# Conv stage of a ConvNeXt-MoE kernel: the choice of experts cut into six parts, and gamma of the stored rows on GpSimd

## The chip, the cores and the metric

The kernel runs on one core of one Trainium2 chip. The metric is the time of one execution on the device in microseconds (us). Before the change it is 4985.2 us, the median of ten runs (4977.12 to 5419.1; nine of the ten lie at or below 4990.11).

Five engines of the core run their own streams of instructions side by side: TensorE (PE in the profile, with its weight loads as PEld), VectorE (DVE), ScalarE (ACT), GpSimd (POOL) and SyncE (SP, which only issues transfers here). They meet through semaphores.

## The reference

Two layers; the change touches the first only. What the first layer computes, in short:

```python
x = depthwise_conv_7x7(input, dw_kernel) + dw_bias        # 32 x 128 x 56 x 56
x = transpose(x, (0, 2, 3, 1))                            # T = 100352 tokens of C = 128 channels
x = (x - mean) / sqrt(var + 1e-6) * ln_gamma + ln_beta    # over the channels of a token
logits = xf @ Wg + bg                                     # 8 experts
topv, topi = top_k(logits, 2); wts = softmax(topv)
# tokens in order of their first weight claim places in the experts, capacity 1.25 * T / 8
h = gelu(eb @ W1 + b1); y = h @ W2 + b2                   # 128 -> 512 -> 128 in each expert
out = input + x + layer_scale * (the two experts' rows, weighted)
```

The second layer (a dilated 3x3 convolution with batch norm, attention on a Fourier transform, gates) follows on that result.

## The kernel before

**Stages.** The conv stage comes first, roughly 0 to 824 us of the span; then the ranking of the tokens, the experts, the return of their rows, and the second layer. Only the conv stage is touched.

**Tiling.** The 100352 tokens are cut into eight groups of 98 columns (`TG`) of 128 tokens. A group's conv result is the SBUF tile `y`, 128 partitions x 98 columns x 128 channels, in float32; there are two of them, so group g + 2 writes where group g lay. One group is convolved in 16 steps (`NS`) of eight channels, each in two halves of four. A half loads its input `xt` on SP's queue (L148; five buffers), runs 32 conv matmuls on TensorE into a PSUM bank `psa` (L157; one of eight banks), and VectorE moves the bank to `y` and adds the bias (L165, called the evacuation). The weights of nine steps stay in SBUF (`stay`), those of the other seven (`wt`) are loaded again for each group (L151).

**What rides along.** All other work on group g is issued among the steps of group g + 1. A group has six blocks of 16 columns and one of two. Each block passes through these phases:

- `stats` (L179): 16 bn_stats (L182), five small VectorE operations (L186 to L192), Sqrt on ScalarE (L193), reciprocal (L194), and the bias `nb` of the normalisation (L195)
- `norm` (L199): 16 activations on ScalarE (L208); in the last group every second one is on VectorE (L203)
- `across` (L219): 16 transposes on TensorE (L225), four evacuations on ScalarE with gamma and beta (L227)
- `affine` (L213): gamma over the block's rows (L214), on VectorE, in the last group on GpSimd; then the store of the rows to `xf` in HBM (L217), 1 MB, issued on ScalarE's queue, in the last group on SP's. Beta is not added here
- `logits` (L234): four matmuls with `Wg` (L237), each for a quarter of the array's columns, and a copy on ScalarE (L246)
- `back` (L248): four transposes (L251) and an addition of the bias on VectorE into `lg` (L254); the small block has L265 and L274 for both phases

`choose` (L283) takes the two best of the eight logits for all 98 columns, and their weights. For each of the two ranks: highest logit (L293), where it is (L294), times reversed index (L297), first such expert (L300); between the ranks the first expert is taken out (L302, L305). Then difference of the two (L316), Exp on ScalarE (L317), and the weights (L318 to L324). These are 16 VectorE instructions and one activation, and ScalarE loads the table of Exp ahead of it and that of Sqrt behind it.

**What sets the order.** `plan` (L332) gives each phase of block b the step min(2b, 11) + d of the next group, with d from `BEHIND` = 0, 1, 3, 4, 4, 6; `choose` comes last, at step 18. There are 16 steps, so what is planned at 16 and later is issued between two groups. In the last group the multiplies and stores are issued behind the steps (`NS` in L340). The Tile framework then places the instructions on the engines and puts in the semaphores, so the order on an engine is near the order of issue, not equal to it. A new group's first evacuation must wait until the stores of the `y` that it overwrites have landed.

Of the kernel before, what the change touches and what calls it, by code (L numbers as in the profile page):

```python
# [30 lines left out]
F32 = mybir.dt.float32  # L31
I32 = mybir.dt.int32
AF = mybir.ActivationFunctionType
ALU = mybir.AluOpType
AX = mybir.AxisListType
# [24 lines left out]
BIG = 1.0e30  # L60
# [14 lines left out]
def conv_seq_kernel(ctx: ExitStack, tc: tile.TileContext, t: dict, out: bass.AP, dbg: dict):  # L75
    nc = tc.nc
# [41 lines left out]
    firsts = [rk.tile([128, FW], F32, name=f"first{r}") for r in (1, 2)]  # L118
    w1, w2 = [rk.tile([128, FW], F32, name=f"w{r}") for r in (1, 2)]

    TG = 2 * NP
    with tc.tile_pool(name="a1", bufs=1) as a1, tc.tile_pool(name="a2", bufs=2) as a2, tc.tile_pool(
        name="a4", bufs=4
    ) as a4, tc.tile_pool(
        name="a5", bufs=5
# [13 lines left out]
        def conv(g, c0, y):  # L139

            stayed = c0 // CB in stays
            if stayed:
                wts = [w[:, stays.index(c0 // CB)] for w in stay]
            else:
                wts = [a2.tile([k, CB, P8 * P8], F32, name=f"wt{b}") for b, k in enumerate(PKS)]
            for c4 in range(0, CB, CX):
                xt = a5.tile([PK, CX, 4 * NCB * NB], F32, name="xt")
                nc.sync.dma_start(out=xt, in_=t["x8"][g, c0 // CB][:, c4 : c4 + CX])  # L148
                if c4 == 0 and (g == 0 or not stayed):
                    for b in range(2):  # L150
                        nc.sync.dma_start(out=wts[b], in_=t[f"wt{b}"][c0 // CB])  # L151
                xv = xt.rearrange("k c (h n q) -> k c h n q", h=2, n=2)
                ps = bank("psa")
                for c in range(4):
                    for b in range(2):
                        for h in range(2):
                            nc.tensor.matmul(  # L157
                                ps[h * 64 : (h + 1) * 64, c * TG : (c + 1) * TG],
                                lhsT=wts[b][:, c4 + c, :],
                                rhs=xv[: PKS[b], c, h, :, b * NB : b * NB + NP],  # L160
                                start=(b == 0),
                                stop=(b == 1),
                            )
                cs = slice(c0 + c4, c0 + c4 + 4)
                nc.vector.tensor_tensor(  # L165
                    out=y[:, :, cs],
                    in0=ps[:, : 4 * TG].rearrange("p (c t) -> p t c", c=4),
                    in1=dwbB[:, cs].unsqueeze(1).broadcast_to([128, TG, 4]),
                    op=ALU.add,
                )  # L170

        def block(g, y, lg, t0, n, end):
# [38 lines left out]


            def affine():  # L213
                (nc.gpsimd if end else nc.vector).tensor_tensor(  # L214
                    out=yb, in0=yb, in1=gB.unsqueeze(1).broadcast_to([128, n, C]), op=ALU.mult
                )
                (nc.sync if end else nc.scalar).dma_start(out=xfv[:, g * TG + t0 : g * TG + t0 + n, :], in_=yb)  # L217

            def across():  # L219
# [40 lines left out]
            else:  # L260
# [12 lines left out]
                def back():  # L273
# [4 lines left out]
                        op=ALU.add,  # L278
                    )

            return [stats, norm, across, affine, logits, back]

        def choose(g, lg):  # L283

            cut = slice(g * TG, (g + 1) * TG)
            bE = [128, TG, E]
            tops = []
            cand = a1.tile(bE, F32, name="cand", tag="cand")
            for r in range(2):

                top = a2.tile([128, TG], F32, name=f"top{r}", tag=f"top{r}")
                first = firsts[r][:, cut]
                nc.vector.tensor_reduce(out=top, in_=lg, axis=AX.X, op=ALU.max)  # L293
                nc.vector.tensor_tensor(  # L294
                    out=cand, in0=lg, in1=top.unsqueeze(2).broadcast_to(bE), op=ALU.is_equal
                )
                nc.vector.tensor_tensor(  # L297
                    out=cand, in0=cand, in1=revi.unsqueeze(1).broadcast_to(bE), op=ALU.mult
                )
                nc.vector.tensor_reduce(out=first, in_=cand, axis=AX.X, op=ALU.max)  # L300
                if r == 0:
                    nc.vector.tensor_tensor(  # L302
                        out=cand, in0=cand, in1=first.unsqueeze(2).broadcast_to(bE), op=ALU.is_equal
                    )
                    nc.vector.scalar_tensor_tensor(  # L305
                        out=lg.rearrange("p t e -> p (t e)"),
                        in0=cand.rearrange("p t e -> p (t e)"),
                        scalar=-BIG,
                        in1=lg.rearrange("p t e -> p (t e)"),
                        op0=ALU.mult,  # L310
                        op1=ALU.add,
                    )
                tops.append(top)

            m1, e1 = tops
            nc.vector.tensor_tensor(out=e1, in0=e1, in1=m1, op=ALU.subtract)  # L316
            nc.scalar.activation(e1, e1, AF.Exp)  # L317
            nc.vector.tensor_scalar(out=e1, in0=e1, scalar1=1.0, scalar2=None, op0=ALU.min)  # L318
            nc.vector.tensor_scalar(out=m1, in0=e1, scalar1=1.0, scalar2=None, op0=ALU.add)
            nc.vector.reciprocal(m1, m1)  # L320
            nc.vector.tensor_scalar(
                out=w1[:, cut], in0=m1, scalar1=0.5, scalar2=1.0, op0=ALU.max, op1=ALU.min
            )
            nc.vector.tensor_tensor(out=w2[:, cut], in0=e1, in1=w1[:, cut], op=ALU.mult)  # L324

        NS = C // CB
        BEHIND = 0, 1, 3, 4, 4, 6
        sizes = [16] * (TG // 16) + ([TG % 16] if TG % 16 else [])  # L330

        def plan(g, y):  # L332

            end = g + 1 == HI // 2
            lg = a2.tile([128, TG, E], F32, name="lg")
            at = {}
            t0 = 0
            for b, n in enumerate(sizes):
                for i, (d, phase) in enumerate(zip(BEHIND, block(g, y, lg, t0, n, end))):
                    at.setdefault(NS if end and i == 3 else min(2 * b, 11) + d, []).append(phase)  # L340
                t0 += n
            at.setdefault(min(2 * b, 11) + BEHIND[-1] + 1, []).append(lambda: choose(g, lg))
            return at

        behind = {}
        for g in range(HI // 2):
            y = a2.tile([128, TG, C], F32, name="y")
            for k in range(NS):
                conv(g, k * CB, y)
                for phase in behind.pop(k, []):  # L350
                    phase()
            for k in sorted(behind):
                for phase in behind[k]:
                    phase()
            behind = plan(g, y)
        for k in sorted(behind):
            for phase in behind[k]:
                phase()

    banks.__exit__(None, None, None)  # L360

# [109 lines left out]
    if True:  # L471
# [39 lines left out]
        for u in range(U):  # L511
            nc.vector.tensor_scalar(
                out=blocks[:, u, :], in0=iota[:R, :NC], scalar1=float(-u), scalar2=None, op0=ALU.add
# [4 lines left out]
            out=token, in0=iota[:R], scalar1=-128.0, scalar2=lane[:R], op0=ALU.add, op1=ALU.add  # L518
# [912 lines left out]
    for pr in range(NI // 2):  # L1431
# [5 lines left out]
        for w in back(pr, *this):  # L1437
# [5 lines left out]
            while fed < goal:  # L1443
                f = next(steps, None)
# [131 lines left out]
```

## Time and profile before

| | |
|---|---|
| median of ten runs | 4985.2 us |
| the profiled execution | 4986.63 us |
| its span | 4984.9 us |
| TensorE busy | 4647.5 us (93%) |
| GpSimd busy | 2606.8 us (52%) |
| VectorE busy | 2802.8 us (56%) |
| ScalarE busy | 2175.2 us (44%) |
| conv matmuls L157 | 4608 records of 263 ns mean |
| gamma L214 on VectorE | 42 of 128 x 2048, 2290 ns mean, and 7 of 128 x 256, 426 ns |
| gamma L214 on GpSimd | 6 of 128 x 2048, about 4.5 us each, and one small one (last group) |
| stores of `xf` | 42 of 1024 KB |

How to read it. The span is cut into stages whose limits differ; the shares are averages over all of them. A timeline line has the start (us from the span's start), the busy time (us), the engine, the line of the kernel with its operation, out<-in by the program's names, the shape (partitions x elements for vector operations), and how many records were joined (x16). A bracket tells how long the engine stood idle before, and what ended that. In a line for a group of instructions, "27.8, 3966" is the busy time in us and the mean of one in ns; the figures behind the second bar are idle time before it. A matmul can appear as two records.

### The profile page before, as it was taken

What the parts mean: (1) busy time and instruction counts of PE and PEld (TensorE: products, weight loads), DVE (VectorE), ACT (ScalarE), POOL (GpSimd) and SP (SyncE); (2) the same over time, 40 slices, a digit from 0 to 9 for tenths busy, and PEclk for the clock granted to TensorE, in tenths of its full rate; (3) what the DMA queues carried; (4) which work ended last, traced back from release to release, by engine and by line L of the source; (5) the groups of instructions that cost most, each with busy time, mean ns of one, the idle gap of its engine ahead of it and who ended that gap; (6) DMA issues with size and microseconds to landing.
All of it is one profiled execution on the core that took longest, in us unless ns stands there. A gap on an engine that the chain in (4) does not pass through costs nothing.

```text
span 4984.9 us, 85712 instructions
## 1 busy us (share of the span) xinstructions
PE 4647.5 (93%) x32980; PEld 3183.2 (64%) x32980; DVE 2802.8 (56%) x5737; ACT 2175.2 (44%) x4258; POOL 2606.8 (52%) x2591
## 2 busy tenths in 40 slices
PE   7999984499989899899999999999999999999998
PEld 6676762376767667677777775666666666555556
DVE  4677678756575756673511233555555555555556
ACT  2666665154534444354455452333333333333333
POOL 0000002354525354567776477777767777777770
PEclk9998896699999999999999999999999999999999
DMA  9887873021212122223333666666666676666662
GB/s 253 236 251 223 233 212 95 23 70 55 69 46 72 53 65 62 59 63 93 98 103 107 202 173 155 177 181 184 184 173 175 187 191 187 182 177 180 183 165 60
DMA packets 767242, 705.13 MB, mean 141 GB/s; under 512 B 72751, under 2 KB 679088, under 8 KB 762740
## 3 DMA queue, kind: packets, MB, share of 16 engines
q1 hardware_dynamic: 596580, 487.54, 33.2%
q0 software_dynamic: 81664, 167.15, 15.1%
q10 hardware_dynamic: 88592, 44.96, 3.1%
q8 instruction: 262, 4.29, 0.4%
q14 instruction: 144, 1.18, 0.1%
HBM read 472.99 MB, written 226.39 MB: 140 GB/s over the span
## 4 chain that ended last, share of the span: by engine, by line
PE 65%; issue 10%; POOL 9%; DVE 9%; DMA 4%; ACT 3%; SPq 0%; DVEq 0%; POOLq 0%; ACTq 0%
PE py L990 14%; PE pf L1185 13%; PE ph L976 12%; PE pm L1236 7%; POOL y L400 5%; PE psa L157 4%; POOL xg L953 4%; PE pt L1228 3%; ACT y L208 2%; PE pyt L225 2%; PE pxt L959 2%; PE pg L1260 2%; PE pre L1325 1%; DVE st L182 1%; PE pxs L1170 1%
## 5 line engine op out<-in xcount | busy, mean ns | idle before, releaser
L400 POOL DMA_INDIRECT y<-yf,slot x1568 | 1567.5, 1000 | 561.3 <-issue 444.0
L953 POOL DMA_INDIRECT xg<-xf,ids x861 | 888.8, 1032 | 834.0 <-DVE ids L878 308.6
L979 ACT ACTIVATE hT<-ph,b1t 128x512 f32<-128x512 f32 (+1 forms) x992 | 676.6, 682 | 1149.1 <-PE ph L976 1123.0
L990 PEld LDWEIGHTS py<-W,hT 128*128 128x128 f32 x7872 | 935.6, 191 | 145.3 <-issue 103.3
L990 PE MATMUL py<-W,hT 128*128 128x128 f32 x7872 | 983.0, 278 | 0.7
L976 PE MATMUL ph<-xT,W 128*128 128x512 f32 (+1 forms) x1984 | 896.4, 591 | 0.0
L1185 PE MATMUL pf<-xp,cw 128*64 128x448 f32 x4032 | 888.3, 550 | 0.3 <-DMA y<-yf,slot 0.3
L1003 DVE TENSOR_TENSOR yo<-py,b2t 128x512 f32<-128x512 f32 (+2 forms) x256 | 170.5, 669 | 714.4 <-issue 562.9
L976 PEld LDWEIGHTS ph<-xT,W 128*128 128x128 f32 x1984 | 357.1, 192 | 333.5 <-issue 329.1
L1185 PEld LDWEIGHTS pf<-xp,cw 128*64 128x64 f32 x4032 | 276.7, 135 | 411.1 <-issue 373.7
L1215 DVE COPY mid<-pt 112x512 f32<-112x512 f32 (+3 forms) x480 | 308.6, 661 | 312.6 <-PE pt L1228 308.4
L214 POOL TENSOR_TENSOR y<-y,gB 128x2048 f32<-128x2048 f32 (+1 forms) x7 | 27.8, 3966 | 781.7 <-PE pyt L225 781.7
L208 ACT ACTIVATE y<-y,nb,sd 128x128 f32<-128x128 f32 x735 | 289.1, 481 | 97.8 <-DVE nb L195 95.7
L1013 ACT ACTIVATE yo<-yo,gates 128x128 f32<-128x128 f32 (+1 forms) x984 | 311.6, 390 | 12.7 <-DVE gates L878 8.8
L1239 ACT COPY T<-pm 128x464 f32<-128x464 f32 (+2 forms) x240 | 124.3, 520 | 375.1 <-PE pm L1236 373.6
L416 DVE TENSOR_TENSOR xa<-xa,y 128x896 f32<-128x896 f32 x224 | 243.7, 1088 | 63.3 <-DMA y<-yf,slot 54.1
L157 PE MATMUL psa<-xt,stay 112*64 112x98 f32 (+1 forms) x4608 | 250.2, 263 | 24.3 <-DMA stay<-in_wt_dram 13.9
L157 PEld LDWEIGHTS psa<-xt,stay 112*64 112x64 f32 (+1 forms) x4608 | 222.3, 145 | 74.8 <-issue 45.3
L165 DVE TENSOR_TENSOR y<-psa,dwbB 128x392 f32<-128x392 f32 x256 | 140.7, 557 | 160.7 <-PE psa L157 159.9
L1174 DVE SCALAR_TENSOR_TENSOR xp<-pxs,beta,xp 128x256 f32<-128x256 f32 x448 | 172.5, 446 | 96.6 <-PE pxs L1170 86.6
L225 PE MATMUL pyt<-ident,y 128*128 128x128 f32 x784 | 173.0, 323 | 54.0 <-ACT y L208 48.8
L959 PE MATMUL pxt<-ident,xg 128*128 128x128 f32 (+1 forms) x984 | 196.2, 278 | 23.9 <-DMA xg<-xf,ids 23.7
(401 smaller groups left out, 6117.0 us busy)
## 6 DMA issues: line engine op xcount, KB each, us to landing
xt<-in_x_dram SPq DMA_DIRECT2D x256, 392.0 KB
yf<-yo SPq DMA_DIRECT2D x240, 256.0 KB
xp<-in_xp_dram SPq DMA_DIRECT2D x32, 1832.0 KB
xa<-xf SPq DMA_DIRECT2D x112, 448.0 KB
xsum<-xa SPq DMA_DIRECT2D x112, 448.0 KB
xs<-xsum SPq DMA_DIRECT2D x112, 448.0 KB
xf<-y ACTq DMA_DIRECT2D x42, 1024.0 KB
y<-yf,slot POOLq DMA_INDIRECT x1568
```

Source lines behind the costliest of these rows:

```text
L157: nc.tensor.matmul(ps[h * 64 : (h + 1) * 64, c * TG : (c + 1) * TG], lhsT=wts[b][:, c4 + c, :], rhs=xv[: PKS[b], c, h, :, b * NB : b * NB ...
L208: nc.scalar.activation(yi, yi, AF.Identity, scale=sd[:, i : i + 1], bias=nb[:, i : i + 1])
L400: behind(nc.gpsimd.indirect_dma_start(out=begun_[r][1][-1][:, m, :], out_offset=None, in_=yf[: 1 + reach(r), :], in_offset=bass.IndirectOf ...
L953: behind(nc.gpsimd.indirect_dma_start(out=xg[:n, q, :], out_offset=None, in_=xf, in_offset=bass.IndirectOffsetOnAxis(ap=ids[:n, c0 + q : c ...
L959: nc.tensor.transpose(pt[:, q * 128 : q * 128 + n], xg[:n, q, :], ident[:n, :n])
L976: nc.tensor.matmul(ph[:, :ns], lhsT=W1[:, e, f * C : (f + 1) * C], rhs=xT[:, :ns], start=True, stop=True)
L979: gelu = nc.scalar.activation(hT[:, f, :ns], ph[:, :ns], AF.Gelu, bias=b1t[:, e, f : f + 1])
L990: nc.tensor.matmul(py[:n, q * C : (q + 1) * C], lhsT=hT[:, f, q * 128 : q * 128 + n], rhs=W2[:, e, f, :], start=(f == 0), stop=(f == FF // ...
L1013: nc.scalar.activation(yo[:n, q], yo[:n, q], AF.Copy, scale=gates[:n, c0 + q : c0 + q + 1])
L1185: step["pe"] = nc.tensor.matmul(pf[i * DD : (i + 1) * DD, : 8 * W], lhsT=cw[:, k, :], rhs=xps[i][:, o : o + 8 * RP].rearrange("p (h w) -> ...
L1215: step["dve"] = nc.vector.tensor_copy(to, of)
L1236: step["pe"] = nc.tensor.matmul(pm[:, i * M : (i + 1) * M], lhsT=mid[:m, i, :], rhs=by, start=True, stop=True)
```

## The change

Three things.

1. `affine` multiplies by gamma on GpSimd for every group. The store becomes a phase of its own, `keep`, with d = 5, a step behind the multiply (d = 4); it is issued on the same queue as before. In the last group both still stand at `NS`.
2. `choose` issues nothing; it returns six parts: highest, earliest, without (take the first expert out), highest, earliest, weigh.
3. `plan` no longer puts the choice at step 18. The six parts of group g's choice are issued at steps 1, 3, 5, 7, 9 and 11 of the plan that holds the phases of group g + 1, that is among the convs of group g + 2, each behind the phases of its step. The parts of the last group are issued at the end.

The computation is the same.

```diff
             def affine():
-                (nc.gpsimd if end else nc.vector).tensor_tensor(
+                nc.gpsimd.tensor_tensor(
                     out=yb, in0=yb, in1=gB.unsqueeze(1).broadcast_to([128, n, C]), op=ALU.mult
                 )
+
+            def keep():
                 (nc.sync if end else nc.scalar).dma_start(out=xfv[:, g * TG + t0 : g * TG + t0 + n, :], in_=yb)
...
-            return [stats, norm, across, affine, logits, back]
+            return [stats, norm, across, affine, logits, back, keep]
...
+            def highest(r):
+                if r == 0:
+                    at["cand"] = a1.tile(bE, F32, name="cand", tag="cand")
+                cand, top = at["cand"], a2.tile([128, TG], F32, name=f"top{r}", tag=f"top{r}")
+                tops.append(top)
                 nc.vector.tensor_reduce(out=top, in_=lg, axis=AX.X, op=ALU.max)
                 nc.vector.tensor_tensor(
                     out=cand, in0=lg, in1=top.unsqueeze(2).broadcast_to(bE), op=ALU.is_equal
                 )
+
+            def earliest(r):
+                cand = at["cand"]
                 nc.vector.tensor_tensor(
                     out=cand, in0=cand, in1=revi.unsqueeze(1).broadcast_to(bE), op=ALU.mult
                 )
...
+            return [
+                lambda: highest(0), lambda: earliest(0), without, lambda: highest(1), lambda: earliest(1), weigh
+            ]
...
-        BEHIND = 0, 1, 3, 4, 4, 6
+        BEHIND = 0, 1, 3, 4, 4, 6, 5
...
-                    at.setdefault(NS if end and i == 3 else min(2 * b, 11) + d, []).append(phase)
+                    at.setdefault(NS if end and i in (3, 6) else min(2 * b, 11) + d, []).append(phase)
                 t0 += n
-            at.setdefault(min(2 * b, 11) + BEHIND[-1] + 1, []).append(lambda: choose(g, lg))
-            return at
+            return at, choose(g, lg)
...
-            behind = plan(g, y)
+            before = parts
+            behind, parts = plan(g, y)
+            for i, part in enumerate(before):
+                behind.setdefault(2 * i + 1, []).append(part)
...
+        for part in parts:
+            part()
```

More of the change, by code (lines that the diff above doesn't have):

```diff
@@ L286, in choose @@
             bE = [128, TG, E]
[L287 to L292, printed above, removed]
+            tops, at = [], {}
+            def highest(r):
[3 more added lines that the diff above has]
+                tops.append(top)
                 nc.vector.tensor_reduce(out=top, in_=lg, axis=AX.X, op=ALU.max)
@@ L299, in choose @@
                 )
[L300 to L323, printed above, removed]
@@ L324, in choose, with without @@
-            nc.vector.tensor_tensor(out=w2[:, cut], in0=e1, in1=w1[:, cut], op=ALU.mult)
+                nc.vector.tensor_reduce(out=firsts[r][:, cut], in_=cand, axis=AX.X, op=ALU.max)
+            def without():
+                cand = at["cand"]
+                nc.vector.tensor_tensor(
+                    out=cand, in0=cand, in1=firsts[0][:, cut].unsqueeze(2).broadcast_to(bE), op=ALU.is_equal
+                )
+                nc.vector.scalar_tensor_tensor(
+                    out=lg.rearrange("p t e -> p (t e)"),
+                    in0=cand.rearrange("p t e -> p (t e)"),
+                    scalar=-BIG,
+                    in1=lg.rearrange("p t e -> p (t e)"),
+                    op0=ALU.mult,
+                    op1=ALU.add,
+                )
@@ new lines, in weigh @@
+            def weigh():
+                m1, e1 = tops
+                nc.vector.tensor_tensor(out=e1, in0=e1, in1=m1, op=ALU.subtract)
+                nc.scalar.activation(e1, e1, AF.Exp)
+                nc.vector.tensor_scalar(out=e1, in0=e1, scalar1=1.0, scalar2=None, op0=ALU.min)
+                nc.vector.tensor_scalar(out=m1, in0=e1, scalar1=1.0, scalar2=None, op0=ALU.add)
+                nc.vector.reciprocal(m1, m1)
+                nc.vector.tensor_scalar(
+                    out=w1[:, cut], in0=m1, scalar1=0.5, scalar2=1.0, op0=ALU.max, op1=ALU.min
+                )
+                nc.vector.tensor_tensor(out=w2[:, cut], in0=e1, in1=w1[:, cut], op=ALU.mult)
@@ L339, in plan @@
                 for i, (d, phase) in enumerate(zip(BEHIND, block(g, y, lg, t0, n, end))):
-                    at.setdefault(NS if end and i == 3 else min(2 * b, 11) + d, []).append(phase)
+                    at.setdefault(NS if end and i in (3, 6) else min(2 * b, 11) + d, []).append(phase)
                 t0 += n
-            at.setdefault(min(2 * b, 11) + BEHIND[-1] + 1, []).append(lambda: choose(g, lg))
-            return at
-        behind = {}
+            return at, choose(g, lg)
+        behind, parts = {}, []
         for g in range(HI // 2):
```

## The prediction

> **What bounds the kernel now.** The profiled execution took 4986.63 us, 1.4 above the median of the ten runs (4985.2) and 1.7 above its own span; every sum below is added to 4986.63. I read the page first: the conv matmuls of L157 hold only 4% of the chain of work that ended last, so the stage can move a small part of the whole. Then the timeline of TensorE for the start of each group's first transposes (L225): 191.19, 283.54, 376.44, 469.99, 565.61, 661.26, a period of 94.0 us on average. The edit acts six times on that period. Its rhythm around one boundary, TensorE:
>
> ```profile
> 457.97 1.54 PE L157 MATMUL psa<-xt,stay 112*64 112x98 f32 x32
> 460.82 1.58 PE L157 MATMUL psa<-xt,stay 112*64 112x98 f32 x32 [1.32 <-DMA xt<-in_x_dram]
> 462.46 2.96 PE L157 MATMUL psa<-xt,wt 112*64 112x98 f32 x64
> 469.99 5.09 PE L225 MATMUL pyt<-ident,y 128*128 128x128 f32 x13 [4.56 <-ACT y L208]
> ```
>
> The last convs of the old group end at 452.44 (P below). TensorE then stands 4.56 us until ScalarE's normalisation (L208) has begun, and 13 transposes take 5.09 us: in the table by stretches the granted clock is 1.00 from 452 to 465, but 0.50 from 470 to 482. ScalarE waits for VectorE:
>
> ```profile
> 463.51 0.29 ACT L317 ACTIVATE top<-top 128x98 f32<-128x98 f32 x1 [12.05 <-DVE top L316]
> 469.44 6.26 ACT L208 ACTIVATE y<-y,nb,sd 128x128 f32<-128x128 f32 x16 [2.14 <-DMA wt<-in_wt_dram]
> ```
>
> VectorE's timeline shows no gap from 452.44 to 469.4: the choice of the group before (L293 to L324) lies among the statistics on which L208 waits.
>
> So a period has two parts. **Boundary**, P to the first gamma multiply (L214): 358.38 to 385.02 and 452.44 to 478.56, 26.4. **Blocks**, first L214 to the next P: 385.02 to 452.44 and 478.56 to 547.81, 68.4, in which blocks follow each other every 10.6 us when TensorE waits for nothing.
>
> **The change part by part.** The order of instructions of the changed kernel is known, its times are not.
>
> *Boundary, choice spread.* A choice is ten VectorE instructions near 0.96 us (0.88 from start to start) and six short ones of 1.7 us together, 10.5 us in the gapless stretch. In the new order only the first reduction and comparison stay ahead of L195 of block 0. VectorE then owes, after P: 0.6 (L165 of P's last half), 15 bn_stats x 0.20, five small operations x 0.10, 2 x 0.87, five evacuations (L165) x 0.48, 0.3 for L194/L195 and 0.4 waiting for Sqrt, together 9.0 us. To this comes a new wait: the first L165 of a group waits for the stores of y two groups back, which in the new order go a step later and behind GpSimd. A 1 MB store issued at 445.69 landed about 7 us later; block 5's multiply ends 2.2 us later than now (4.50 for 2.29), and its store then queues behind four L227 evacuations on ScalarE. Behind the waiting L165 stand ten bn_stats and all other evacuations. I take 2.3 us, about the lateness of the multiply; ends 0 (it lands in time) and 6.4 (its packets took 4.1 us, 448.5 to 452.6, while few loads ran; at half that rate beside the loads of the boundary, where the DMA share is 1.05, they take 4.1 more). On SP's queue, the two loads of step 3 and the weights of step 6 wait in the new order for these stores too; five xt buffers and a distance of three steps (9 us) cover that, so I cost it at 0, and its price without cover is the same 4.1. Normalisation starts at P + 11.3 instead of P + 17.0; 16 normalisations take 6.3, the transposes keep up at full clock, and the multiply starts 1.0 later: 18.6. **Gain 26.4 - 18.6 = 7.8** (ends 3.7 and 10.1). Two table loads of 1.28 us on ScalarE merely move; they now come while it has slack.
>
> *Blocks, logits matmuls.* In the new order, four of six large blocks have their four L237 matmuls split by conv matmuls into runs of 2, 1, 1: 14 runs a group instead of seven. Two forms of this are in the trace:
>
> ```profile
> 140.31 1.05 PE L237 MATMUL plq<-yT,wg 128*32 128x512 f32 x4 [0.17 <-DVE y L165]
> 141.30 0.72 PE L157 MATMUL psa<-xt,stay 112*64 112x98 f32 x10
> 141.95 1.05 PE L237 MATMUL plq<-yT,wg 128*32 128x512 f32 x2
> 142.93 0.73 PE L157 MATMUL psa<-xt,stay 112*64 112x98 f32 x12
> 143.59 1.05 PE L237 MATMUL plq<-yT,wg 128*32 128x512 f32 x2
> ```
>
> ```profile
> 435.45 1.07 PE L237 MATMUL plq<-yT,wg 128*32 128x512 f32 x8
> ```
>
> (A count of 8 is four matmuls in two records each.) A run of one costs as much as a run of four, 0.98 from start to next start. L237 held TensorE 15.74 us in group 1, which is split already, and 7.43 in later groups; blocks of group 1 follow each other every 12.93 us. So eight runs x 0.98 - one run saved or covered = +7 to +7.8. With four block periods of 12.8, 10.0 ahead of them and 8.1 behind, blocks have a floor of 69.3: the 68.4 of now holds 6 us of half clock and waits that the new boundary spares.
>
> *Blocks, gamma on GpSimd.* The last group does this already:
>
> ```profile
> 755.66 4.50 POOL L214 TENSOR_TENSOR y<-y,gB 128x2048 f32<-128x2048 f32 x1 [755.21 <-PE pyt L225]
> 764.40 4.49 POOL L214 TENSOR_TENSOR y<-y,gB 128x2048 f32<-128x2048 f32 x1 [4.24 <-PE pyt L225]
> ```
>
> ```profile
> 756.20 0.25 DVE L194 RECIPROCAL sd<-sd 128x16 f32<-128x16 f32 x1
> 756.35 0.25 DVE L182 BATCH_NORM_STATS2 st<-y 128x6 f32<-128x128 f32 x1
> 756.50 3.70 DVE L195 SCALAR_TENSOR_TENSOR nb<-nb,sd 128x16 f32<-128x16 f32 x1
> ...
> 764.49 4.43 DVE L192 TENSOR_TENSOR sd<-sd,df 128x16 f32<-128x16 f32 x1
> ```
>
> VectorE loses 6 x 2.29 of its own multiply a group. But operations with two inputs from SBUF (L192, L195), elsewhere 0.15 to 0.25 us, end with GpSimd's multiply; bn_stats and reciprocal run beside it. One is caught per multiply, for 4.4 us at most. What queues behind it is the next L165, so a PSUM bank, so the convs; and in the new order the first conv of an odd step needs a bank freed only about 3 us before. VectorE's sum a group (32 evacuations, 98 bn_stats, small ones, choice) is 53.6 + 6 x 3.5 caught = 75, below 88 to 95, so it delays rather than bounds. Walking through the new order block by block: block 1's normalisation starts late behind its L195, 1.3; the evacuation behind it 1.3; block 2, where choice operations also queue, 3.0 (1.5 to 5); the last block, a one-input operation of the choice (L203 beside GpSimd took 4.62, so such are caught too), 1.9. Sum 7.5; ends 0 (L192 and L195 always ahead of the multiply) and 13.2 (2.2 in all six). Blocks become 69.3 + 7.5 = 76.8: **+8.4**.
>
> Here a rule bears. Row first: while GpSimd multiplied at 848.41 (1.26 us), a VectorE operation from PSUM plus one SBUF operand took 0.16 us, one from two SBUF operands (L656) 1.03. The Trainium skill, "SBUF — State Buffer", section "Who interferes with whom", says that only the port shared by both engines is exclusive, so the evacuations L165 would go free. That row is only three columns wide. By the rule the evacuations cost nothing; were they caught too, I would add 27 us over the stage. The skill's "Perfetto Trace Analysis", section "Optimizing Scalar/DVE Operations", warns that moving work between these two engines may bring nothing because of that port; by it alone the multiply's move would be worth 0.
>
> *Rest.* Group 1 has no earlier choice and is split already; its multiplies on GpSimd cost +1 (0 to 4). The end of the stage (734.5 to 823.8) has VectorE busy 84.4 of 89.3 us and the last choice only in other positions: 0, within 3. DMA's own floor, 22.1 MB a group at 270 GB/s, is 82 us, below both periods. Nothing behind the stage changes.
>
> Sum: 6 x (8.4 - 7.8) + 1 = +4.6, **4991.2**.
>
> **Rivals.**
> - *B, slower: VectorE falls behind in the blocks.* Every multiply catches L192 or L195 early and each catch delays a bank, the upper end 13.2 plus about 1.3 of half clock where TensorE waits over 4 us (after the 4.56 it lost 6): 5.7 + 1.3 = +7 beyond A a group, 4991.2 + 42 = 5033; at half that 5012. For it: all six multiplies of the last group caught one, 25.2 us in all. Against it: TensorE has banks ahead. It decides from 1.5 us lost per multiply.
> - *C, faster: spread as meant.* L195 is through before each multiply, stalls vanish, the boundary gain is whole: 6 x (0.9 - 7.8) + 1 = -40, 4946; halfway 4967. For it: group 1, without choice at its start and with split logits, took 72.3 from first transposes to P at clock 1.00, later groups 74 to 78. Against it: the caught rows.
> - *D: the late store takes the choice's place at the boundary*: wait 6.4, gain 3.7: 6 x (8.4 - 3.7) + 1 = +29, 5016. For it: loads fill DMA at the boundary. Against it: stores now land 7 to 8 us after issue, with or without loads beside them.
>
> **How the numbers follow.** A (even trade, 4975 to 5008) 0.42, B 0.26, C 0.24, D 0.08. The range 4946 to 5033 reaches to the middle estimates of B and C and leaves out the outer parts of both, about 0.15. About 0.2% (10 us) is what a measurement can tell from no change. Faster: C and 0.05 of A, 0.29. Slower: B, D and 0.13 of A, 0.47. Same: 0.24.
>
> **What would show it.** The wait of 4.6 us for L208 at boundaries gone and clock near 1.00 there (boundary); L237's busy time near 14 us a group (split); L192/L195 above 3 us in groups 2 to 6, with TensorE idle on L165 behind them (stalls); the first L165 of a group waiting for a store (D). P to multiply not near 18.6, or blocks outside 73 to 81, makes the sum wrong.

## The result and the profile after

The changed kernel takes 5018.53 us (median of eight runs, 5013.74 to 5020.9) beside 4983.44 us for the kernel before: a ratio of 1.0069, with a 95% interval of 1.006 to 1.0078. It is slower by about 35 us; the forecast was +4.6, inside a range of 4946 to 5033. The profiled execution took 5022.68 us, 36.05 more than that of before.

Where the 36 us lie, by landmarks of TensorE's timeline. P is the time at which TensorE begins the convs of the next group. The prediction calls 452.44 the end of the old group's convs; its lines show that these end at 451.48 and that 452.44 is the start of the new ones. Its sums all use the start, so they stand. For the last group P is the end of its convs.

| part | before | after | measured | predicted |
|---|---|---|---|---|
| first P (groups 0 and 1) | 173.84 | 181.26 | +7.4 | +1 |
| boundary, P to first L214, mean of six | 26.3 | 18.1 | -8.2 | -7.8 |
| blocks, first L214 to next P, mean of six | 67.2 | 79.7 | +12.5 | +8.4 |
| the six groups together | 560.6 | 586.9 | +26.3 | +3.6 |
| last conv to last choice | 89.5 | 94.5 | +5.0 | 0 |
| rest of the kernel | | | -2.7 | 0 |

The boundary did what was forecast. ScalarE's timeline at the same boundary as was shown of before; P is now at 383.40:

```profile
389.90 0.31 ACT L193 ACTIVATE sd<-sd,eps 128x16 f32<-128x16 f32 x1 [9.91 <-DVE sd L192]
392.30 2.03 ACT L208 ACTIVATE y<-y,nb,sd 128x128 f32<-128x128 f32 x5 [2.10 <-DVE nb L195]
```

Normalisation starts 8.9 us after P (17.0 before), and TensorE no longer stands 4.56 us for it. In the table by stretches (TensorE, its weight loads, VectorE, ScalarE and GpSimd busy, granted clock, DMA share, GB/s) the clock is 1.00 over that boundary:

```profile
383.40:400.00 16.60, 15.92 (x295) 14.14 (x296) 16.12 (x64) 8.00 (x20) 0.00 (x0) 1.00 1.01 268
```

The loss is in the blocks. GpSimd's timeline for blocks 1 and 2, and VectorE's beside it:

```profile
409.66 4.52 POOL L214 TENSOR_TENSOR y<-y,gB 128x2048 f32<-128x2048 f32 x1 [5.10 <-PE pyt L227]
423.82 4.52 POOL L214 TENSOR_TENSOR y<-y,gB 128x2048 f32<-128x2048 f32 x1 [9.64 <-PE pyt L227]
```

```profile
410.05 4.17 DVE L195 SCALAR_TENSOR_TENSOR nb<-nb,sd 128x16 f32<-128x16 f32 x1
414.14 0.55 DVE L165 TENSOR_TENSOR y<-psa,dwbB 128x392 f32<-128x392 f32 x1
...
424.45 3.92 DVE L192 TENSOR_TENSOR sd<-sd,df 128x16 f32<-128x16 f32 x1
```

Both held operations end when the multiply ends, at 414.2 and 428.3, and the evacuation L165 queues behind. TensorE in the same stretch:

```profile
414.75 0.72 PE L157 MATMUL psa<-xt,stay 112*64 112x98 f32 x10 [1.40 <-DVE y L165]
...
426.45 1.05 PE L239 MATMUL plq<-yT,wg 128*32 128x512 f32 x4
431.03 0.72 PE L157 MATMUL psa<-xt,stay 112*64 112x98 f32 x10 [3.52 <-DVE y L165]
431.68 1.17 PE L239 MATMUL plq<-yT,wg 128*32 128x512 f32 x2
432.78 1.25 PE L157 MATMUL psa<-xt,stay 112*64 112x98 f32 x12
433.95 1.92 PE L239 MATMUL plq<-yT,wg 128*32 128x512 f32 x2
```

Here both costs of a block are seen: the logits in runs of 2, 1, 1, and the wait of 3.52 us for an evacuation, after which a logits matmul takes up to twice as long (the last line: 1.92; a run of one took 1.05 before the change). The table by stretches shows the lower granted clock, 0.65, behind that wait (before it: 1.00):

```profile
431.00:435.80 4.80, 4.77 (x27) 1.80 (x27) 3.26 (x21) 4.80 (x14) 0.00 (x0) 0.65 0.01 5
```

The third wait is at the end of the group, behind the one-input operation L326 of the choice, which ends at 471.6 with GpSimd's multiply of 467.01 to 471.5 (VectorE, then TensorE):

```profile
468.28 3.33 DVE L326 TENSOR_SCALAR top<-top 128x98 f32<-128x98 f32 x1
```

```profile
473.56 5.49 PE L157 MATMUL psa<-xt,wt 112*64 112x98 f32 x64 [2.49 <-DVE y L165]
```

### The profile page after: what moved, and what is told of

It is laid out like the page before. It is cut to its first block, busy times and chain, and to the rows that moved or that the text cites. A ratio compares the mean times of both kernels' runs of the same rounds, so it can differ in the third digit from the quotient of the medians.

```text
span 5020.9 us, 85643 instructions
## 1 busy us (share of the span) xinstructions
PE 4666.5 (93%) x32980; PEld 3193.1 (64%) x32980; DVE 2788.9 (56%) x5688; ACT 2177.9 (43%) x4258; POOL 2810.8 (56%) x2640
## 3 DMA queue, kind: packets, MB, share of 16 engines
q0 software_dynamic: 81664, 167.15, 14.9%
## 4 chain that ended last, share of the span: by engine, by line
PE 67%; DVE 10%; issue 10%; POOL 8%; DMA 3%; ACT 1%; SPq 0%; DVEq 0%; POOLq 0%; ACTq 0%
PE py L1006 14%; PE pf L1201 13%; PE ph L992 13%; PE pm L1252 7%; POOL y L416 5%; PE psa L157 5%; PE pt L1244 3%; POOL xg L969 3%; DVE st L182 2%; PE pxt L975 2%; PE pg L1276 2%; PE plq L239 2%; PE pre L1341 1%; PE pxs L1186 1%; PE pyt L227 1%
## 5 line engine op out<-in xcount | busy, mean ns | idle before, releaser
L214 POOL TENSOR_TENSOR y<-y,gB 128x2048 f32<-128x2048 f32 (+1 forms) x56 | 224.8, 4018 | 623.1 <-PE pyt L227 500.3
L165 DVE TENSOR_TENSOR y<-psa,dwbB 128x392 f32<-128x392 f32 x256 | 143.1, 559 | 307.1 <-PE psa L157 297.6
L157 PE MATMUL psa<-xt,stay 112*64 112x98 f32 (+1 forms) x4608 | 260.9, 263 | 46.9 <-DVE y L165 26.8
L157 PE MATMUL psa<-xt,wt 112*64 112x98 f32 (+1 forms) x3584 | 207.0, 265 | 30.4 <-DVE y L165 20.7
```

Of the source, the lines that this page charges most:

```text
L157: nc.tensor.matmul(ps[h * 64 : (h + 1) * 64, c * TG : (c + 1) * TG], lhsT=wts[b][:, c4 + c, :], rhs=xv[: PKS[b], c, h, :, b * NB : b * NB ...
```

## The experiments

Theories, named in the expectations: T1 is the prediction's, with the half clock seen above added (boundary gained; blocks lost to operations held by GpSimd's multiply, to half clock behind the waits, and to the split logits). Rivals: R1, the parts crowd VectorE; R2, the split is the whole loss; later T2 and R3 to R5. Three chips were used. On two of them the kernel before takes 6220 and 6244 us, with longer stages behind the conv stage; so the measure is the ratio to the kernel before on the same chip, and the stage times of the trace. Those are comparable: a full step of convs, 64 records, is 2.95 us on all three.

Summary, means in us (logits: L237 of before, busy time for 100 us between 300 and 600):

| kernel | gamma | choice | store | boundary | blocks | logits | ratio to before (95%) |
|---|---|---|---|---|---|---|---|
| before | VectorE | boundary | with multiply, ScalarE's queue | 26.3 | 67.2 | 7.8 | 1 |
| after (second run: c_after) | GpSimd | parts | a step later, ScalarE's | 18.1 | 79.7 | 15.8 | 1.007 (1.0053 to 1.0087) |
| e1_parts_only | VectorE | parts | a step later, ScalarE's | 25.4 | 68.9 | 9.0 | 0.9994 (0.9981 to 1.0008) |
| e2_gpsimd_only | GpSimd | boundary | with multiply, ScalarE's | 26.1 | 74.4 | 17.3 | 1.0066 (1.0046 to 1.0086) |
| e5_no_lock | GpSimd | drawn together | a step later, ScalarE's | 32.2 | 70.0 | 14.9 | 1.0078 (1.005 to 1.0106) |
| e6_parts_early | VectorE | parts | multiply's step, ScalarE's | 18.2 | 68.6 | 15.1 | 0.9916 (0.9895 to 0.9938) |
| e12_keep_step_earlier | GpSimd | parts | multiply's step, ScalarE's | 16.8 | 71.5 | 18.6 | 0.996 (0.9946 to 0.9974) |
| e7_parts_pool_store | VectorE | parts | GpSimd's queue | 17.2 | 63.4 | 12.1 | **0.9827** (0.9811 to 0.9844) |
| e8_after_pool_store | GpSimd | parts | GpSimd's queue | 17.1 | 71.4 | 9.6 | 0.9928 (0.9911 to 0.9945) |
| e10_before_pool_store | VectorE | boundary | GpSimd's queue | 27.4 | 62.2 | 8.5 | 0.9932 (0.9905 to 0.996) |
| e11_two_operands_psum | GpSimd | parts | GpSimd's queue | 17.7 | 68.8 | 10.9 | 0.9921 (0.99 to 0.9943) |

**One part alone.** e1_parts_only:

```diff
-                nc.gpsimd.tensor_tensor(
+                (nc.gpsimd if end else nc.vector).tensor_tensor(
```

> Choice in six parts as in the changed kernel, gamma back on VectorE except in the last group. Theory T1 (the boundary gain of the parts is real, the loss comes from VectorE operations caught behind GpSimd's multiply, the half clock after the waits of TensorE, and the split logits, which this order does not have in groups 3 to 7): boundary near 18 us, blocks 62 to 65 us, faster than before, 4915 to 4945 us. Rival R1 (the parts themselves crowd VectorE among the blocks): no faster than before, 4990 us or more, with TensorE waiting for evacuations as now.

Ratio 0.9994: R1's figure, not T1's. But the trace (its execution was 24 us above that kernel's median) shows no crowding in the blocks. It shows a boundary of 25.4 us where 18 was expected, and VectorE at the start of a group:

```profile
457.47 1.25 DVE L182 BATCH_NORM_STATS2 st<-y 128x6 f32<-128x128 f32 x6
466.50 0.57 DVE L165 TENSOR_TENSOR y<-psa,dwbB 128x392 f32<-128x392 f32 x1 [7.79 <-DMA xf<-y]
```

The first evacuation waits 7.8 us (9.1 and 8.8 at other boundaries) for the store of the old `y`. Block 5's store was issued a step late, at 451.49, the small block's at 454.19, and P is 457.07. This is the prediction's rival D, in a kernel that has not GpSimd's delay. T1's sum for this kernel is wrong; T2 (the last store ends the boundary once the choice is gone) takes its place and is tested by e6, e7 and e10.

e2_gpsimd_only:

```diff
-                (nc.gpsimd if end else nc.vector).tensor_tensor(
+                nc.gpsimd.tensor_tensor(
```

> The kernel before with one word changed: gamma on GpSimd in every group, choice at the boundary. T1: catches and split stay, the boundary's 26 us and its half clock come back: slower than the changed kernel, 5050 to 5085 us. R1: without parts among the blocks most of the loss is gone, 4980 to 5005 us.

Ratio 1.0066, between the two. Gamma on GpSimd costs 7.2 us of blocks a group without any choice among the blocks; it also splits the logits (17.3 for 7.8), so this edit is enough for a split. It is not the only one that makes it: e6 below has gamma on VectorE and 15.1. From here to the changed kernel the blocks lose another 5.3, and the boundary gains 8.0; that step adds the parts and the later store, and e12 below shows that the loss goes with the store, not with the parts.

**The split.** e4_whole_logits, the four matmuls in a critical section:

```diff
+                    with tc.tile_critical():
                         for k in range(4):
                             nc.tensor.matmul(
```

> The changed kernel with the four logits matmuls of a block kept together on TensorE (same work, other order). T1: L239's busy time falls from about 16 to 7.4 us a group, but part of it was slack in which VectorE caught up, so the waits for evacuations stay or grow: 4975 to 5000 us. Rival R2 (the split alone makes the loss): 8 x 0.98 us x 6 groups and more gone, 4970 us or less.

Ratio 1.0463 (1.044 to 1.0487), and inconclusive. The section keeps the four together, but also makes TensorE wait before each four for work that the matmuls don't need (TensorE's timeline):

```profile
289.84 0.38 PE L157 MATMUL psa<-xt,stay 112*64 112x98 f32 x2
296.27 1.93 PE L240 MATMUL plq<-yT,wg 128*32 128x512 f32 x8 [6.05 <-DMA xt<-in_x_dram]
```

**The hold.** e5_no_lock: the changed kernel with statistics and softmax temporaries in PSUM, in short

```diff
-                st = a2.tile([128, n, 6], F32, name="st", tag="st")
+                st = spare[:, at0 : at0 + n * 6].rearrange("p (t s) -> p t s", s=6)      # spare: one PSUM bank
...
+                nc.vector.tensor_copy(so, st[:, :, 4:6])
...
-                nc.vector.tensor_tensor(out=sd, in0=sd, in1=df, op=ALU.add)
+                nc.vector.tensor_tensor(out=sd, in0=dq, in1=sd, op=ALU.add)              # dq in PSUM
```

> The changed kernel, with the statistics and the softmax of the choice rewritten so that none of their two-input VectorE operations reads two operands from SBUF: one operand each goes through a PSUM bank (7 banks remain for the rest), at two more short VectorE instructions a block. GpSimd's multiply and the split logits stay. T1: no operation is held for 3 to 4 us, the 7.4 us of waits a group and the half clock after them go, also in group 1: 4945 to 4980 us. R1 or R2: within 10 us of the changed kernel, 5008 us or more.

The total says R1 or R2; the stage times say why. No small operation is above 0.3 us any more, multiplies follow each other every 12.7 us (the split's own pace), and blocks fall from 79.7 to 70.0: T1's part is there, though not by itself, since the choice had left the blocks. For the order that came out for this kernel puts ten of the parts' long instructions back ahead of block 0's L201, so the boundary grew to 32.2; at 390.26 a first evacuation also waited 4.9 us for a store. An edit of the temporaries had moved the choice too, which made this a poor test of the total. e11 below repeats it with the parts in place.

**The store.** c_after, the changed kernel again:

> The changed kernel once more, beside the three that follow, as their common measure: 30 to 40 us slower than the kernel before on the same chip, blocks near 80 us, boundary near 18 us.

As before, 5019.81 us, and the same stage times within 0.1 us. e6_parts_early is e1 with `BEHIND`'s last number changed from 5 to 4:

> Choice in six parts, gamma on VectorE, and the store issued in the multiply's step (d = 4), not a step later. In this order groups 3, 5 and 7 have whole logits, groups 2, 4 and 6 split ones. Theory T2 (with the choice gone from the boundary, what ends last there is the landing of the last stores, on which a group's first evacuation waits; a step earlier they land in time): that wait falls from 8 to 9 us to 2 or less, boundary 18 to 20 us; blocks 62 to 64 us where the logits are whole and 69 to 71 where they are split; 30 to 55 us faster than the kernel before. Rival R1 (the parts give nothing in themselves): within 8 us of the kernel before.

42 us faster. T2's boundary is right in the mean (18.2), but four of the six are shorter (15.3 to 17.8) and two longer (24.4 and 20.4). The longest still has the wait for the stores (VectorE, P at 424.83):

```profile
432.86 0.57 DVE L165 TENSOR_TENSOR y<-psa,dwbB 128x392 f32<-128x392 f32 x1 [6.38 <-PE psa L157]
```

The profile names TensorE, but the convs of that half had ended at 426.42; the last packet of the queue that carries the stores ended at 431.89. The blocks are not as T2 said: 67 to 70 us in all groups, since the logits stayed largely split (15.1).

e7_parts_pool_store:

```diff
-            def keep():
-                (nc.sync if end else nc.scalar).dma_start(out=xfv[:, g * TG + t0 : g * TG + t0 + n, :], in_=yb)
+                (nc.sync if end else nc.gpsimd).dma_start(out=xfv[:, g * TG + t0 : g * TG + t0 + n, :], in_=yb)
```

(inside `affine`, which is on VectorE, with `keep` out of `BEHIND` as well).

> Choice in six parts, gamma on VectorE, stores issued with the multiply but on GpSimd's queue, where nothing stands ahead of them; the order on TensorE then has whole logits in nearly all blocks. T2: the best of all, boundary 18 to 20 us, blocks 62 to 66 us, 45 to 70 us faster than the kernel before. R1: within 8 us.

4896.58 us, the best of all, and 1.7% below the kernel before and 2.5% below c_after; its 86 us are more than T2's 45 to 70. The logits are not whole in nearly all blocks (12.1). The period is 80.6 us, less than the 82 us that the prediction took for the DMA's floor at 270 GB/s; it was not a floor. From the first P to the last conv TensorE is busy 478.7 of 483.7 us:

```profile
163.35:647.02 483.67, 478.71 (x7182) 376.22 (x7181) 389.47 (x1253) 372.81 (x834) 45.94 (x42) 0.98 0.92 274
```

e8_after_pool_store is the same with gamma on GpSimd:

> The changed kernel with the stores issued behind the multiply on GpSimd's own queue; the order on TensorE then has whole logits in five of six large blocks. T1: operations of VectorE are still held by GpSimd's multiply, TensorE still waits for evacuations, blocks 70 to 75 us: from 5 us slower to 20 us faster than the kernel before. Rival R2 (the split is the whole loss): no waits of more than 1 us left, blocks 62 to 66 us, 40 us or more faster than the kernel before.

T1's blocks: 71.4 with mostly whole logits, against 63.4 in e7. The total, 34 us faster than the kernel before, lies between T1's 20 and R2's 40. The price of GpSimd's multiply in this order is 8.0 us a group: TensorE is busy 68.5 us of the blocks for 63.2, at a granted clock of 0.93 to 0.95 (e7: 0.94 to 1.00), and the other 2.7 us it stands idle. The groups of VectorE's operations (busy us, mean ns of one), first e8, then e7:

```profile
L195 DVE SCALAR_TENSOR_TENSOR nb<-nb,sd 128x16 f32<-128x16 f32 x41 | 66.7, 1627 | 0.5
L324 DVE TENSOR_SCALAR top<-top 128x98 f32<-128x98 f32 x6 | 18.5, 3089 | 0.0
```

```profile
L195 DVE SCALAR_TENSOR_TENSOR nb<-nb,sd 128x16 f32<-128x16 f32 x42 | 6.9, 164 | 0.1
L324 DVE TENSOR_SCALAR top<-top 128x98 f32<-128x98 f32 x6 | 1.2, 205 | 0.0
```

VectorE gives up 96.1 us of multiplies and loses 77 us held in these two lines alone.

e10_before_pool_store, the kernel before with `nc.gpsimd` in place of `nc.scalar` in the store:

> The kernel before with one word changed: stores issued on GpSimd's queue; choice at the boundary, gamma on VectorE. Theory T2 (the boundary is set by the choice, and only without it does an early store pay): boundary 25 to 27 us as before, blocks 63 to 67 us: 0 to 25 us faster than the kernel before. Rival R3 (the queue of the stores, not the parts, makes the gain of the best variant so far): 50 us or more faster.

The boundary is the choice's (27.4); ratio 0.9932, 38 us by the medians on that chip, more than T2 allowed and less than R3. So the store on GpSimd's queue gives 3.8 us a group (5.0 in the blocks, less 1.1 at the boundary), and the parts then give 9.0 more (e10 to e7: boundary 27.4 to 17.2, blocks 62.2 to 63.4).

e11_two_operands_psum, e8 with two temporaries in PSUM:

```diff
-                nc.vector.tensor_tensor(out=nb, in0=me, in1=mo, op=ALU.add)
+                nc.vector.tensor_tensor(out=sm, in0=me, in1=mo, op=ALU.add)      # sm in PSUM
...
-                    out=nb, in0=nb, scalar=-0.5, in1=sd, op0=ALU.mult, op1=ALU.mult
+                    out=nb, in0=sm, scalar=-0.5, in1=sd, op0=ALU.mult, op1=ALU.mult
```

> Gamma on GpSimd, choice in parts and stores on GpSimd's queue as in e8_after_pool_store; in addition two temporaries of the statistics lie in one PSUM bank (7 are left for the rest), so that the sum of variance and the bias of the normalisation read one operand from SBUF instead of two. The number of instructions is the same. T1 (GpSimd's multiply holds VectorE operations with two SBUF operands, and that alone is its price): L196 and L199 stay at 0.2 us, blocks fall from 71.4 to 64 to 68 us (the softmax's one-input operation and the three short ones ahead can still be held), 4905 to 4930 us. Rival R4 (the multiply's price is its length, through late stores or through everything on VectorE running slower): blocks stay above 70 us, 4940 us or more.

```profile
L305 DVE TENSOR_TENSOR cand<-cand,revi 128x784 f32<-128x784 f32 x12 | 31.7, 2645 | 0.0
L191 DVE TENSOR_TENSOR spare<-st 128x16 f32<-128x16 f32 x41 | 25.8, 628 | 0.1
L191 DVE TENSOR_TENSOR spare<-st 128x2 f32<-128x2 f32 x7 | 19.1, 2725 | 0.0
L196 DVE TENSOR_TENSOR sd<-spare,sd 128x16 f32<-128x16 f32 x41 | 6.8, 165 | 0.2
L199 DVE SCALAR_TENSOR_TENSOR nb<-spare,sd 128x16 f32<-128x16 f32 x41 | 6.7, 164 | 0.5
```

The two operations with an operand in PSUM are free as T1 says (0.165 us beside the same multiplies), and the blocks fall, but only to 68.8: VectorE runs on to the next operation with two SBUF operands (L191, L305), and that one is held. T1's kind is right, its size here was too large. The total shows no gain that can be told from e8's: 0.9921 for 0.9928, with intervals that overlap.

e12_keep_step_earlier, one number in the changed kernel:

```diff
-        BEHIND = 0, 1, 3, 4, 4, 6, 5
+        BEHIND = 0, 1, 3, 4, 4, 6, 4
```

> The changed kernel with one number changed: stores issued at d = 4, in the multiply's step, still on ScalarE's queue. T1: the stores hardly bound the changed kernel, since TensorE comes to the boundary late; ScalarE, which issues them, waits for the multiply instead: boundary 16 to 20 us, blocks 77 to 82 us, 20 to 40 us slower than the kernel before. Rival R5 (the late store is its loss): 0 or faster than the kernel before.

T1's expectation failed: ratio 0.996, 22 us faster than before. R5's figure is right, but its cause is not the landing of a store (the longest wait of an evacuation for one is 0.7 us). The boundary hardly moves (16.8 for 18.1); the blocks fall from 79.7 to 71.5, with the logits more split than ever (18.6). What changed is VectorE's order: in five of the six groups L195 of blocks 2 to 5 stands behind 14, 18, 22 and 26 evacuations of the next group, in the changed kernel behind 12, 16, 20 and 24. A multiply then starts at 407.31, the evacuations due go ahead, and VectorE reaches L195 only as the multiply ends:

```profile
410.26 0.24 DVE L194 RECIPROCAL sd<-sd 128x16 f32<-128x16 f32 x1
410.54 1.34 DVE L195 SCALAR_TENSOR_TENSOR nb<-nb,sd 128x16 f32<-128x16 f32 x1
```

1.3 us instead of 4.2, with no evacuation due behind it. TensorE's waits for evacuations over the stage (us in total, times, longest), first the changed kernel, then e12:

```profile
PE psa L157 <- DVE y L165: 46.2, 18, 5.1
```

```profile
PE psa L157 <- DVE y L165: 9.9, 8, 2.8
```

**The three parts of the change apart.** Boundary and blocks together are a group's period; the table gives what each part is worth beside different others, always with the order of instructions that came with it.

- Store a step later: costs 7.5 us a group with gamma on VectorE (e6 to e1) and 9.5 with gamma on GpSimd (e12 to after).
- Gamma on GpSimd: costs 7.0 (before to e2) and 8.0 (e7 to e8), but 1.5 in the order of e6 to e12.
- Choice in parts: gains 6.7 (before to e6), 12.2 (e2 to e12) and 9.0 (e10 to e7), and nothing when the store goes late with it (before to e1).

With the store left in the multiply's step, the other two parts together gain 5.2 us a group (before to e12). The later store makes the change a loss: at the boundary where TensorE comes in time (e1), and by another order on VectorE where it does not (after).

## Why the prediction was right in kind and wrong in size

The forecast of +4.6 was rival A's, and 31 us of the measured time are missing in it. The time came out near the prediction's D (5016) and half of B (5012); only the width of the range holds it.

- **Boundary: right, in part by luck.** -8.2 for -7.8, though in other terms: normalisation starts at P + 8.9 here and P + 10.2 a group later (11.3 was summed). The 2.3 us taken for the late store at every boundary were 0 at five and over 5 at one. At three boundaries the first evacuation stood 1.3 us, until TensorE, at half clock, had ended the first half of its convs. At the first (P at 181.26) it was the store, so D holds there (VectorE):

```profile
190.07 1.04 DVE L165 TENSOR_TENSOR y<-psa,dwbB 128x392 f32<-128x392 f32 x2 [5.43 <-DMA xt<-in_x_dram]
```

The load that the profile names had long been used (the convs of that half ended at 182.85); the stores were issued at 178.21 and later, and the last packet of their queue ended at 188.77. At the other boundaries the store was not late because TensorE was: it had lost its time in the blocks before. e1 shows what the same store costs when TensorE is not late (D, 7.5 to 9.1 us at five boundaries).
- **Split: right.** L239 is busy 15.8 of 100 us for 7.8, and multiplies without a wait between them follow each other every 12.69 us (12.8 was taken).
- **Holds: right.** The waits of TensorE for evacuations are 1.4 to 1.5, 3.5 and 2.5 us in five of the six groups, 7.4 together; the prediction summed 7.5 over four places, of which these are three (its fourth, block 1's late normalisation, stopped ScalarE and not TensorE). Two evacuations L165 inside the multiply of 400.01 to 404.56 took 0.57 and 0.55, so the rule of the Trainium skill ("SBUF — State Buffer", "Who interferes with whom") holds for 392 columns from PSUM as it did for three, and its 27 us were rightly left out. The other page's warning ("Perfetto Trace Analysis", "Optimizing Scalar/DVE Operations"), that such a move might not help, is too mild for this case: from e7 to e8 the move costs 8.0 us a group.
- **Missed: half clock behind the waits.** The step that failed is the blocks' sum, "69.3 + 7.5 = 76.8". It charges a wait with its own length only. In the group from 400.01 to 480.88 the floor is 68.5 (9.65, four of 12.69, 8.1), the waits 7.4, and the remaining 4.9 are matmuls at half clock: about 1.6 after the 3.52 us wait and 3.3 after the 2.49. The prediction had such a term in B alone, at 1.3.
- **Missed: the base.** 68.4 came from two groups (their times give 68.3); the mean of six is 67.2. That is 1.2 us a group.
- **Mis-sized: group 1**, "+1 (0 to 4)". Its second multiply (112.75) held L188 for 4.53, and TensorE waited 5.09 us, half clock behind it: +7.4. **The end of the stage**, "0, within 3": +5.0; I did not separate its causes.

The sum with measured terms is 6 x (12.5 - 8.2) + 7.4 + 5.0 - 2.7 = 35.5, for 36.05 by the two executions. B's mechanism (held operations that delay a bank, half clock behind the waits) made the sign, with waits of A's size. The prediction priced the later store only by its landing, at the boundary; e12 shows that without it the same mechanism costs far less.

What stays open: why one number or one queue changes which logits are split and where L195 stands. The order is the scheduler's, and no run here shows how it comes about.

## What to carry to other kernels

Work moved from VectorE to GpSimd is paid here by whatever VectorE operation with two SBUF operands, or one-input operation such as L326, comes up during it (up to 4.5 us each), and by everything in line behind it; where nothing is due behind it, it costs little (e12). Look at the order of both engines, not at their busy shares: here VectorE was relieved of 2.29 us a block and the stage lost time. When a wait at a stage's boundary is taken away, ask what is late next. Here it was a store, and the change had moved just that store a step back; the parts were worth nothing with the late store (e1) and 6.7 to 12.2 us a group with an early one. And a reordering on one engine can come with a reordering on another: compare the orders of all engines before an effect is put down to an edit.

## What the runs showed of the hardware that was not expected

The same wait, on the same instruction, was followed by different clocks. Six groups have the wait of 2.49 us in the last block; three of the stretches from there to P:

```profile
377.88:383.40 5.52, 5.52 (x73) 5.23 (x73) 1.56 (x5) 1.28 (x1) 0.00 (x0) 0.69 0.79 237
473.56:480.88 7.32, 7.32 (x72) 6.76 (x72) 1.56 (x5) 1.28 (x1) 0.00 (x0) 0.50 0.76 218
570.25:574.17 3.92, 3.92 (x72) 3.63 (x72) 1.57 (x5) 1.28 (x1) 0.00 (x0) 1.00 0.99 280
```

Same 72 or 73 matmul records, granted clock (the last but two) 0.69, 0.50 and 1.00, and 5.52, 7.32 and 3.92 us. The Trainium skill's page "TensorE: Matmul & The Clock Gate", section "What's actually happening", puts the fall behind an idle window of some 3.4 us, and says that this window is free-running. No run here shows the window itself; different clocks behind equal waits would fit one that does not start with the wait. As a least length of the wait, 3.4 us does not hold here: 2.49 us was enough in five of the six groups. So the length of a wait alone does not tell its price: here it was up to 3.4 us more than the wait (7.32 for 3.92).
